# Mixture-of-experts blocks of 256, 192, 128 or 64 tokens, in nested branches, with two groups of TensorE's columns for the parts of 64

## The chip, the cores and the metric

The kernel runs on one core of one Trainium2 chip. The core has five instruction streams that run beside each other and meet through semaphores: TensorE (PE in the profile; its weight loads are listed as PEld), VectorE (DVE), ScalarE (ACT), GpSimd (POOL) and SyncE (SP). SyncE issues plain DMA transfers, GpSimd the indirect ones, which gather or scatter rows by a list of row numbers. The metric is the device time of one execution in microseconds (us). Before the change it was 790.62 us, the median of three runs (790.05 to 791.95).

## The reference

One block of a transformer with adaptive layer norm, all in float32, on 4 sequences of 1024 tokens of width D = 256 (T = 4096 tokens in all). The first half is a gated linear recurrence in place of attention, the second a mixture of E = 8 experts of hidden width F = 1024, of which each token uses its best two:

```python
def ffn(x, Wg, bg, W1, b1, W2, b2):
    gate_scores = softmax(x @ Wg + bg)
    topk_scores, topk_idx = top_k(gate_scores, 2)
    topk_scores = topk_scores / (sum(topk_scores) + 1e-08)
    combine_w = ...            # (tokens, E): the two scores at their experts, else 0
    for e in range(8):
        h = gelu(x @ W1[e] + b1[e])
        output += (h @ W2[e] + b2[e]) * combine_w[..., e:e+1]

h = layernorm(x) * (1 + ca) + sa
x = x + ga * recurrence(h)             # projections, associative scan, projection back
h = layernorm(x) * (1 + cb) + sb
x = x + gb * ffn(h)
```

The modulation rows sa, ca, ga, sb, cb, gb come from a small product of the condition c. Which tokens go to which expert is known only on the chip, after the gate.

## The kernel before

**First part, to about 301 us.** The sequences are worked through in eight chunks of 512 tokens (lines 1020 to 1116): norm, four projections (L417), scan, output projection (L454), the second norm and the gate (`f_gate`, L564, a product whose four groups of 32 tokens go to four groups of 32 columns of TensorE). The normalized rows and the gate rows `gb` are stored in a table `hx` in memory, the sum so far in the output. After each sequence the routing functions (`r_*`) find the two experts of each token and its rank within each expert. GpSimd scatters pairs (token, weight) into `lists` in memory, one region of T entries per expert, a few at a time (`drain`, L586).

**Blocks.** Each expert's list is cut into blocks of TK = 256 tokens; a block is two halves of 128 (HK = 2). There are up to NJ = 39 blocks. Which expert and which place of its list a block has stands in small tables that VectorE computes: `full_table` for blocks 0 to 7 and 8 to 15, which are certain to be whole, and `late_table` (L765) for the other 23. The late table has two segments of eight columns: first the whole blocks of each expert (a remainder of over 128 makes one more whole block), then a half block for each remainder of 1 to 128. `table` finds block i's segment by comparing its number with the running sum over all columns (operations on 23 x 16 elements). The two ends, the number of whole blocks and of all blocks, are loaded into registers of every engine as `n_whole` and `n_blocks`.

**Work of block j.** SyncE loads the entries of block j+3 (`fetch_entries`), GpSimd gathers the rows of block j+2 (`fetch_rows`, L830, three buffers `hb`), SyncE loads the expert's weights for block j+2 (`fetch_weights`: w1 and w2 of 1 MB each, two biases; three buffers, one of them in space freed by the first part, named proj and wo_sb in the profile). `b_up` (L917) makes h = gelu(w1 x + b1): 16 products on TensorE (L928; float32, each shows as two records in the profile), the gelu on ScalarE (L937). `b_turn` (L898) turns the next block's rows with 16 transposes on VectorE (L915), so that its up can start at once. `b_down` (L952) makes, for each half, 8 products with the hidden values as weights and w2 as the moving side (L958, 16 records); VectorE adds the bias (L972) and multiplies by the token's weight and gate row (L973), and GpSimd adds the rows to the output by a scatter (L945).

**Order.** The engines' order is the order of the code (the kernel is under a manual schedule, all engines). Blocks 0 to 27 (`sure_whole` = 28) are whole in any case and have no branch. From block 28 on, `work_either` (L1152) puts the whole form and the half form of a block into the two sides of an If on `n_whole` (compare-and-branch at L1153), and every engine has both sides in its program, one after the other. `sure` = 32 blocks exist in any case; beyond, `rest` (L1202) nests one If per block on `n_blocks` (L1203). `fetch_used` (L875) asks the same for block j+2's rows and weights. From block 31 on, a block's last part is kept back: its rows stay in `last_y` and their places in `last_at` (copied at L968), and the scatter is issued inside the next `rest`, or at the end. So this copy waits until the scatter of the block before has landed.

Of the kernel before, what the change touches and what calls it, by code (L numbers as in the profile page):

```python
# [9 lines left out]
F32 = mybir.dt.float32  # L10
# [9 lines left out]
def tile_adaln_block(  # L20
# [688 lines left out]
    def table(counts, starts, segments, n, what):  # L709
# [6 lines left out]
        past = small.tile([P, n, sg], F32, tag="past", name=f"past{what}", bufs=1)  # L716
# [18 lines left out]
        if sg > E:  # L735
            nc.vector.tensor_scalar(at, who, float(E), float(-E), ALU.is_ge, ALU.mult)
            nc.vector.tensor_add(who, who, at)
# [4 lines left out]
    counts2 = const.tile([P, 2, E], F32, tag="counts2", name="counts2")  # L742
    starts = const.tile([P, 2 * E + 1], F32, tag="starts", name="starts")
# [5 lines left out]
    nc.gpsimd.memset(starts[:, 2 * E :], float(E * BPE))  # L749
# [15 lines left out]
    def late_table():  # L765

        whole = blocks_of(float(P - 1), "lw")
        some = blocks_of(float(TK - 1), "ls")
        nc.vector.tensor_sub(counts2[:, 0, :], whole, done)
        nc.vector.tensor_sub(counts2[:, 1, :], some, whole)  # L770
        nc.vector.tensor_add(starts[:, E : 2 * E], starts[:, :E], counts2[:, 0, :])
        tab, cum = table(
            counts2.rearrange("p s e -> p (s e)"), starts, 2 * E, NJ - NM, "l"
        )
        ends_at = small.tile([P, 2], I32, tag="ends_at", name="ends_at", bufs=1)
        nc.vector.tensor_scalar_add(ends_at[:, 0:1], cum[:, E - 1 : E], float(NM))
        nc.vector.tensor_scalar_add(ends_at[:, 1:2], cum[:, 2 * E - 1 :], float(NM))
        return tab, ends_at
# [22 lines left out]
    def seen(j: int):  # L801

        return next((batches * S for n, batches, _ in TIERS if j < n), T)
# [71 lines left out]
    def fetch_used(j: int, half: bool):  # L875

        if j + 3 < NJ:
            fetch_entries(j + 3)

        def rest():  # L880
            fetch_rows(j + 2, half)
            fetch_weights(j + 2)

        if j + 2 < sure:
            rest()
        elif j + 2 < NJ:
            with tc.If(n_blocks > j + 2):
                rest()
# [28 lines left out]
    def b_up(j: int, half: bool = False):  # L917
        w1, bb, xT = (BK[j][n] for n in ("w1", "bb", "xT"))
        g = xpool.tile([P, FC, TK], F32, tag="g", name=f"g_{j}_{half}", bufs=1)
        BK[j]["g"] = g  # L920
        n = P if half else TK
        at_once = TB // n
        for f2 in range(FC // at_once):
            ph = ps_mm.tile([P, at_once, n], F32, tag="mm", name=f"ph_{j}_{f2}_{half}")
# [16 lines left out]
    last_y = xpool.tile([P, D], F32, tag="last_y", name="last_y", bufs=1)  # L941
    last_at = const.tile([P, 1], I32, tag="last_at", name="last_at")
# [9 lines left out]
    def b_down(j: int, half: bool = False, mid=None, keep: bool = False):  # L952

        g, w2, b2b, ent, hb = (BK[j][n] for n in ("g", "w2", "b2b", "ent", "hb"))
        for t in range(1 if half else HK):
            py = ps_y.tile([P, D], F32, tag="y", name=f"pye_{j}_{t}_{half}")
            for fc in range(FC):
                nc.tensor.matmul(  # L958
                    py,
                    lhsT=g[:, fc, ts(t, P)],  # L960
                    rhs=w2[:, fc, :],
                    start=(fc == 0),
                    stop=(fc == FC - 1),
                )
            kept_back = keep and t == (0 if half else HK - 1)
            if kept_back:
                yb, at = last_y, last_at
                nc.vector.tensor_copy(last_at, ent[:, t, 0:1])  # L968
            else:
                yb = xpool.tile([P, D], F32, tag="yb", name=f"yb_{j}_{t}_{half}", bufs=3)  # L970
                at = ent[:, t, 0:1]
            nc.vector.tensor_add(yb, py, b2b)  # L972
            nc.vector.scalar_tensor_tensor(  # L973
                yb, yb, ent[:, t, 1:2].bitcast(F32), hb[:, t, D:], ALU.mult, ALU.mult
# [5 lines left out]
            ins = add_rows(yb, at, seen(j))  # L980
# [162 lines left out]
    def work(j: int, half: bool = False, keep: bool = False):  # L1143
        if j >= sure_whole:
            fetch_used(j, half)
        b_up(j, half)
        if j + 1 < NJ:

            b_turn(j + 1, half)
        b_down(j, half, keep=keep)  # L1150

    def work_either(j: int, keep: bool = False):  # L1152
        with tc.If(n_whole > j) as whole:  # L1153
            work(j, False, keep)
        with whole.Else():
            work(j, True, keep)


    sure_whole = (2 * T - E * P) // TK
    sure = 2 * T // TK  # L1160
    for j in range(2, sure_whole):
# [31 lines left out]
    n_whole = nc.values_load(  # L1193
        ends_at[0:1, 0:1], min_val=sure_whole, max_val=NJ, skip_runtime_bounds_check_because=why
    )
    n_blocks = nc.values_load(
        ends_at[0:1, 1:2], min_val=sure, max_val=NJ, skip_runtime_bounds_check_because=why
    )
    for j in range(sure_whole, sure):
        work_either(j, j == sure - 1)  # L1200

    def rest(j: int):  # L1202
        with tc.If(n_blocks > j):  # L1203
            add_rows(last_y, last_at, T)
            work_either(j, True)
            if j + 1 < NJ:
                rest(j + 1)


    rest(sure)  # L1210
# [34 lines left out]
```

## Time and profile before

| | |
|---|---|
| time, median of three runs | 790.62 us (790.05 to 791.95) |
| the profiled execution's own time | 789.1 us |
| its span, first to last instruction | 787.4 us |
| TensorE busy | 772.8 us, 98% of the span |
| mean granted clock of TensorE | 0.997 of full speed |
| VectorE, ScalarE, GpSimd busy | 504.3, 241.7, 290.3 us |
| TensorE, last whole block (30) | 728.26 to 742.07 us |
| TensorE, five half blocks (31 to 35) | 742.07 to 777.6 us |
| last scatter, issued and landed | 778.93 and 782.65 us |

The profile is that of one execution. Its lines give the engine, the line of the kernel, the operation, what it writes and reads, the shape (partitions x elements) and the number of instructions or records. Names such as `ph_True` carry the flag `half`: True for a half block. The letter q behind an engine (PEldq, SPq) marks instructions of its sequencer: branches, semaphores, issues of DMAs. Queue q8 carries the instructions of TensorE, in packets of 16 KB, q14 those of other engines.

### The profile page before, as it was taken

How to read it: one execution, taken by the hardware profiler on the slowest of the kernel's cores; microseconds unless marked ns; L12 is line 12 of the kernel's file. 1: busy time of each engine (PE TensorE's matmuls, PEld its weight loads, DVE VectorE, ACT ScalarE, POOL GpSimd, SP SyncE). 2: the span in 40 equal slices, each digit the busy share in tenths (PEclk: the TensorE clock that was granted, in tenths of full speed). 3: DMA queues.
4: the chain of work that ended last, by engine and by line, in shares of the span. 5: the costliest groups of instructions: out<-in, count | busy, mean ns of one | idle time of the engine just before them, and what ended most of it. 6: DMA issues, size and time to landing. Idle time of an engine off the chain costs nothing.

```text
span 787.4 us, 10804 instructions
## 1 busy us (share of the span) xinstructions
PE 772.8 (98%) x3279; PEld 577.1 (73%) x3279; DVE 504.3 (64%) x1391; ACT 241.7 (31%) x560; POOL 290.3 (37%) x370
## 2 busy tenths in 40 slices
PE   8999999999999999999999999999999999999995
PEld 5455545454546557888888888888888888888994
DVE  5787877898789869767547453544536354453563
ACT  4434243534433343223222122221312222131231
POOL 2102010106142712456564564634434243343431
PEclk9999999999999999999999999999999999999998
DMA  8321334042313265799469898898878687885781
GB/s 296 95 70 47 116 102 142 23 127 86 100 55 113 55 185 183 241 328 258 73 161 206 249 247 253 245 294 223 235 211 230 186 235 217 218 232 167 221 264 25
DMA packets 116040, 138.13 MB, mean 175 GB/s; under 512 B 25782, under 2 KB 100090, under 8 KB 115968
## 3 DMA queue, kind: packets, MB, share of 16 engines
q1 hardware_dynamic: 97184, 111.46, 45.0%
q0 software_dynamic: 17216, 25.25, 15.9%
q10 hardware_dynamic: 1568, 0.57, 0.3%
q8 instruction: 32, 0.52, 0.3%
q14 instruction: 40, 0.33, 0.1%
HBM read 113.52 MB, written 25.42 MB: 176 GB/s over the span
## 4 chain that ended last, share of the span: by engine, by line
PE 83%; DMA 8%; DVE 4%; issue 2%; POOL 1%; ACT 1%; POOLq 0%; DVEq 0%
PE ph_False L928 25%; PE pye_False L958 23%; PE pya L454 7%; PE pk L417 6%; PE pgi L417 6%; PE pu L417 6%; PE pgo L417 6%; DMA hb<-hx,ent 5%; DMA out_dram<-yb_False,ent 2%; PE idle L263 1%; DMA proj<-in_L_ffn_W_dram 1%; PE pm L290 1%; PE pta L399 1%; PE pl L564 1%; DVE s L443 0%
## 5 line engine op out<-in xcount | busy, mean ns | idle before, releaser
L937 ACT ACTIVATE g_False<-ph_False,bb 128x256 f32<-128x256 f32 x248 | 103.8, 470 | 303.0 <-issue 188.2
L915 DVE STREAM_TRANSPOSE xT<-hb 32x128 f32<-32x128 f32 (+1 forms) x576 | 168.8, 293 | 12.7 <-DMA hb<-hx,ent 3.6
L958 PE MATMUL pye_False<-w,g_False 128*128 128x256 f32 x672 | 148.7, 379 | 0.0
L928 PE MATMUL ph_False<-xT,w 128*128 128x256 f32 x672 | 148.6, 379 | 0.0
L928 PEld LDWEIGHTS ph_False<-xT,w 128*128 128x128 f32 x672 | 127.4, 190 | 17.9 <-issue 0.7
L958 PEld LDWEIGHTS pye_False<-w,g_False 128*128 128x128 f32 x672 | 127.5, 190 | 17.6 <-issue 0.2
L945 POOL DMA_INDIRECT out_dram<-yb_False,ent x46 | 73.4, 1595 | 139.9 <-DVE yb_False L973 138.4
L972 DVE TENSOR_TENSOR yb_False<-pye_False,b2b 128x256 f32<-128x256 f32 x42 | 17.8, 424 | 126.3 <-PE pye_False L958 123.8
L586 POOL DMA_INDIRECT lists<-pay,placei x64 | 66.4, 1037 | 38.5 <-DMA ent<-lists 27.4
L928 PE MATMUL ph_False<-xT,proj 128*128 128x256 f32 x320 | 70.8, 379 | 0.7 <-DMA proj<-in_L_ffn_W_dram 0.7
L958 PE MATMUL pye_False<-proj,g_False 128*128 128x256 f32 x320 | 70.7, 379 | 0.0
L928 PEld LDWEIGHTS ph_False<-xT,proj 128*128 128x128 f32 x320 | 60.7, 190 | 9.3 <-DVE yb_False L972 1.0
L958 PEld LDWEIGHTS pye_False<-proj,g_False 128*128 128x128 f32 x320 | 60.8, 190 | 8.3
L830 POOL DMA_INDIRECT hb<-hx,ent x53 | 55.6, 1048 | 22.4 <-issue 15.6
L417 PE MATMUL pk<-hT,proj 128*128 128x512 f32 x128 | 61.0, 599 | 0.7 <-ACT hT L1015 0.7
L223 POOL TENSOR_TENSOR rstd_f<-rstd_f,expo 128x4 f32<-128x4 f32 x8 | 8.2, 1022 | 142.4 <-DVE rstd_f L222 98.8
L417 PE MATMUL pu<-hT,proj 128*128 128x512 f32 x128 | 60.2, 592 | 0.0
L417 PE MATMUL pgo<-hT,proj 128*128 128x512 f32 x128 | 60.2, 592 | 0.0
L417 PE MATMUL pgi<-hT,proj 128*128 128x512 f32 x128 | 60.2, 592 | 0.0
L454 PE MATMUL pya<-wo,z 128*128 128x256 f32 x256 | 56.8, 380 | 0.0
L454 PEld LDWEIGHTS pya<-wo,z 128*128 128x128 f32 x256 | 48.4, 190 | 8.6 <-issue 2.4
L972 DVE TENSOR_TENSOR yb_False<-pye_False,wo_sb 128x256 f32<-128x256 f32 x20 | 8.5, 424 | 60.4 <-PE pye_False L958 60.3
(234 smaller groups left out, 811.1 us busy)
## 6 DMA issues: line engine op xcount, KB each, us to landing
w<-in_L_ffn_W_dram SPq DMA_DIRECT2D x48, 1024.0 KB
proj<-in_L_ffn_W_dram SPq DMA_DIRECT2D x24, 1024.0 KB
hx<-gb SPq DMA_DIRECT2D x4, 1024.0 KB
out_dram<-x SPq DMA_DIRECT2D x8, 512.0 KB
hx<-h SPq DMA_DIRECT2D x8, 512.0 KB
x<-in_L_attn_x_dram SPq DMA_DIRECT2D x7, 512.0 KB
swapped<-u SPq DMA_DIRECT2D x7, 512.0 KB
hT<-swapped SPq DMA_DIRECT2D x28, 128.0 KB
```

The source lines that it names most:

```text
L223: nc.gpsimd.tensor_tensor(rstd, rstd, expo[:, 0, :], ALU.pow)
L263: nc.tensor.transpose(idle[:, :P], ident, ident)
L417: nc.tensor.matmul(ps, lhsT=w[:, k, col : col + P], rhs=hT[:, k, :], start=(k == 0), stop=(k == KC - 1),)
L454: nc.tensor.matmul(py[:, t, :], lhsT=z[hc][:, ts(2 * q + t, P)], rhs=wo[:, hc, :], start=(hc == 0), stop=(hc == HC - 1),)
L586: ins = nc.gpsimd.indirect_dma_start(out=lists[:, :], out_offset=IndirectOffsetOnAxis(ap=place, axis=0), in_=what, in_offset=None, bounds_ ...
L830: nc.gpsimd.indirect_dma_start(out=hb[:, t, :], out_offset=None, in_=hx[: seen(j), :], in_offset=IndirectOffsetOnAxis(ap=BK[j]["ent"][:, t ...
L915: nc.vector.transpose(to[ts(q, SQ), :, :, ts(i, SQ)], hb[ts(i, SQ), :, :, ts(q, SQ)])
L928: nc.tensor.matmul(ph[:, u, :], lhsT=w1[:, k, ts(fc, P)], rhs=xT[:, k, :n], start=(k == 0), stop=(k == KC - 1),)
L937: nc.scalar.activation(g[:, fc, :n], ph[:, u, :], AF.Gelu_apprx_tanh, bias=bb[:, fc : fc + 1])
L945: return nc.gpsimd.indirect_dma_start(out=out_rows[:n], out_offset=IndirectOffsetOnAxis(ap=at, axis=0), in_=yb, in_offset=None, bounds_che ...
L958: nc.tensor.matmul(py, lhsT=g[:, fc, ts(t, P)], rhs=w2[:, fc, :], start=(fc == 0), stop=(fc == FC - 1),)
L972: nc.vector.tensor_add(yb, py, b2b)
```

## The change

The blocks of the late table get four sizes, 256, 192, 128 and 64 tokens, instead of two. An expert's remainder takes the smallest size that holds it. The table has four segments of eight columns (its scratch space moves into spare columns of wo_sb), and four limits `n_upto` are loaded instead of two. `sure(k)` gives for each size the smallest and the largest value of its limit, (26, 33), (28, 35), (30, 37), (32, 39); branches start at block 26 instead of 28, and `work_any` nests one If for each further size that a block number may have: two sizes at 26 and 27, three at 28 and 29, four at 30 to 32, and fewer beyond. All sizes that are possible for a block stand in every engine's program one after the other, smaller ones behind larger ones; TensorE's program grows from 541 to 616 KB.

A block of 192 is a part of 128 and one of 64. For a part of 64 tokens the products of `b_down` alternate between PSUM's partitions 0 to 63 and 64 to 127, each by its own group of 64 columns of TensorE (`beside` = 2); a second addition on VectorE joins the two sums. Operations behind it work on 64 partitions. `last_y` is cleared once, early, since a part of 64 fills only half of it; in the scatter that is kept back the other rows go where `last_at` says.

```diff
         tab = small.tile([P, 2, n], I32, tag=f"tab{what}", name=f"tab{what}", bufs=1)
-        past = small.tile([P, n, sg], F32, tag="past", name=f"past{what}", bufs=1)
+        if what == "l":
+            past = wo_sb.rearrange("p c d -> p (c d)")[:, D : D + n * sg]
+            past = past.rearrange("p (n s) -> p n s", s=sg)
+        else:
+            past = small.tile([P, n, sg], F32, tag="past", name=f"past{what}", bufs=1)
         who = small.tile([P, n], F32, tag="who", name=f"who{what}", bufs=1)
...
         nc.vector.tensor_scalar_min(tab[:, 1, :], at, float(E * BPE))
-        if sg > E:
+        for _ in range(sg // E - 1):
             nc.vector.tensor_scalar(at, who, float(E), float(-E), ALU.is_ge, ALU.mult)
...
-    counts2 = const.tile([P, 2, E], F32, tag="counts2", name="counts2")
-    starts = const.tile([P, 2 * E + 1], F32, tag="starts", name="starts")
+    QT = P // 2
+    sizes = [TK, TK - QT, P, QT]
+    NS = len(sizes)
...
+    counts4 = const.tile([P, NS, E], F32, tag="counts4", name="counts4")
+    starts = const.tile([P, NS * E + 1], F32, tag="starts", name="starts")
     done = const.tile([P, E], F32, tag="done", name="done")
...
     nc.gpsimd.memset(starts[:, E : E + 1], float(E * BPE))
-    nc.gpsimd.memset(starts[:, 2 * E :], float(E * BPE))
+    nc.gpsimd.memset(starts[:, NS * E :], float(E * BPE))
...
-        whole = blocks_of(float(P - 1), "lw")
-        some = blocks_of(float(TK - 1), "ls")
-        nc.vector.tensor_sub(counts2[:, 0, :], whole, done)
-        nc.vector.tensor_sub(counts2[:, 1, :], some, whole)
-        nc.vector.tensor_add(starts[:, E : 2 * E], starts[:, :E], counts2[:, 0, :])
+        upto = [
+            blocks_of(float(TK - 1 - (sizes[k + 1] if k + 1 < NS else 0)), f"l{k}")
+            for k in range(NS)
+        ]
+        for k in range(NS):
+            nc.vector.tensor_sub(counts4[:, k, :], upto[k], upto[k - 1] if k else done)
+        for k in range(1, NS):
+            nc.vector.tensor_add(
+                starts[:, k * E : (k + 1) * E], starts[:, (k - 1) * E : k * E],
+                counts4[:, k - 1, :],
+            )
         tab, cum = table(
-            counts2.rearrange("p s e -> p (s e)"), starts, 2 * E, NJ - NM, "l"
-        )
-        ends_at = small.tile([P, 2], I32, tag="ends_at", name="ends_at", bufs=1)
-        nc.vector.tensor_scalar_add(ends_at[:, 0:1], cum[:, E - 1 : E], float(NM))
-        nc.vector.tensor_scalar_add(ends_at[:, 1:2], cum[:, 2 * E - 1 :], float(NM))
+            counts4.rearrange("p s e -> p (s e)"), starts, NS * E, NJ - NM, "l"
+        )
+        ends_at = small.tile([P, NS], I32, tag="ends_at", name="ends_at", bufs=1)
+        nc.vector.tensor_scalar_add(
+            ends_at, cum.rearrange("p (s e) -> p s e", e=E)[:, :, E - 1], float(NM)
+        )
         return tab, ends_at
...
-        if j + 2 < sure:
+        if j + 2 < sure_any:
             rest()
         elif j + 2 < NJ:
-            with tc.If(n_blocks > j + 2):
+            with tc.If(n_upto[-1] > j + 2):
                 rest()
...
-    def b_up(j: int, half: bool = False):
+    def b_up(j: int, n: int = TK):
         w1, bb, xT = (BK[j][n] for n in ("w1", "bb", "xT"))
-        g = xpool.tile([P, FC, TK], F32, tag="g", name=f"g_{j}_{half}", bufs=1)
+        g = xpool.tile([P, FC, TK], F32, tag="g", name=f"g_{j}_{n}", bufs=1)
         BK[j]["g"] = g
-        n = P if half else TK
-        at_once = TB // n
+        at_once = min(TB // n, FC // 2)
         for f2 in range(FC // at_once):
-            ph = ps_mm.tile([P, at_once, n], F32, tag="mm", name=f"ph_{j}_{f2}_{half}")
+            ph = ps_mm.tile([P, at_once, n], F32, tag="mm", name=f"ph_{j}_{f2}_{n}")
             for u in range(at_once):
...
     last_y = xpool.tile([P, D], F32, tag="last_y", name="last_y", bufs=1)
+    nc.gpsimd.memset(last_y, 0.0)
     last_at = const.tile([P, 1], I32, tag="last_at", name="last_at")
...
-    def b_down(j: int, half: bool = False, mid=None, keep: bool = False):
+    def b_down(j: int, size: int = TK, mid=None, keep: bool = False):
         g, w2, b2b, ent, hb = (BK[j][n] for n in ("g", "w2", "b2b", "ent", "hb"))
-        for t in range(1 if half else HK):
-            py = ps_y.tile([P, D], F32, tag="y", name=f"pye_{j}_{t}_{half}")
+        parts = [(0, min(size, P))] + ([(1, size - P)] if size > P else [])
+        for t, n in parts:
+            py = ps_y.tile([P, D], F32, tag="y", name=f"pye_{j}_{t}_{size}")
...
+            beside = P // n
             for fc in range(FC):
                 nc.tensor.matmul(
-                    py,
-                    lhsT=g[:, fc, ts(t, P)],
+                    py[ts(fc % beside, n), :],
+                    lhsT=g[:, fc, ds(t * P, n)],
                     rhs=w2[:, fc, :],
-                    start=(fc == 0),
-                    stop=(fc == FC - 1),
+                    start=(fc < beside),
+                    stop=(fc >= FC - beside),
                 )
-            kept_back = keep and t == (0 if half else HK - 1)
+            kept_back = keep and (t, n) == parts[-1]
             if kept_back:
...
             else:
-                yb = xpool.tile([P, D], F32, tag="yb", name=f"yb_{j}_{t}_{half}", bufs=3)
+                yb = xpool.tile([P, D], F32, tag="yb", name=f"yb_{j}_{t}_{size}", bufs=3)
                 at = ent[:, t, 0:1]
-            nc.vector.tensor_add(yb, py, b2b)
+            nc.vector.tensor_add(yb[:n], py[:n], b2b[:n])
+            if beside > 1:
+                nc.vector.tensor_add(yb[:n], yb[:n], py[n:])
             nc.vector.scalar_tensor_tensor(
-                yb, yb, ent[:, t, 1:2].bitcast(F32), hb[:, t, D:], ALU.mult, ALU.mult
+                yb[:n], yb[:n], ent[:n, t, 1:2].bitcast(F32), hb[:n, t, D:], ALU.mult, ALU.mult
             )
...
                 nc.gpsimd.memset(between, 0.0)
-            ins = add_rows(yb, at, seen(j))
+            ins = add_rows(yb[:n], at[:n], seen(j))
             for other in BK[j]["acc"]:
...
-    def work(j: int, half: bool = False, keep: bool = False):
-        if j >= sure_whole:
-            fetch_used(j, half)
-        b_up(j, half)
+    def sure(k: int):
...
+        less = sizes[k + 1] if k + 1 < NS else 0
+        return (
+            (2 * T - E * less) // TK,
+            max((2 * T - p * (less + 1)) // TK + p for p in range(E + 1)),
+        )
...
+    def work(j: int, size: int, keep: bool):
+        fetch_used(j, size <= P)
+        b_up(j, size)
         if j + 1 < NJ:
-            b_turn(j + 1, half)
-        b_down(j, half, keep=keep)
...
-    def work_either(j: int, keep: bool = False):
-        with tc.If(n_whole > j) as whole:
-            work(j, False, keep)
-        with whole.Else():
-            work(j, True, keep)
...
-    sure_whole = (2 * T - E * P) // TK
-    sure = 2 * T // TK
+            b_turn(j + 1, size <= P)
+        b_down(j, size, keep=keep)
...
+    def work_any(j: int, keep: bool):
...
+        able = [
+            k for k in range(NS) if j < sure(k)[1] and (k == 0 or j >= sure(k - 1)[0])
+        ]
...
+        def choose(i: int):
+            k = able[i]
+            if i == len(able) - 1:
+                work(j, sizes[k], keep)
+                return
+            with tc.If(n_upto[k] > j) as first:
+                work(j, sizes[k], keep)
+            with first.Else():
+                choose(i + 1)
...
+        choose(0)
...
+    sure_whole, sure_any = sure(0)[0], sure(NS - 1)[0]
+    assert sure(NS - 1)[1] == NJ
     for j in range(2, sure_whole):
...
-    n_whole = nc.values_load(
-        ends_at[0:1, 0:1], min_val=sure_whole, max_val=NJ, skip_runtime_bounds_check_because=why
-    )
-    n_blocks = nc.values_load(
-        ends_at[0:1, 1:2], min_val=sure, max_val=NJ, skip_runtime_bounds_check_because=why
-    )
-    for j in range(sure_whole, sure):
-        work_either(j, j == sure - 1)
+    n_upto = [
+        nc.values_load(
+            ends_at[0:1, k : k + 1], min_val=sure(k)[0], max_val=NJ,
+            skip_runtime_bounds_check_because=why,
+        )
+        for k in range(NS)
+    ]
+    n_blocks = n_upto[-1]
+    for j in range(sure_whole, sure_any):
+        work_any(j, j == sure_any - 1)
...
             add_rows(last_y, last_at, T)
-            work_either(j, True)
+            work_any(j, True)
             if j + 1 < NJ:
...
-    rest(sure)
+    rest(sure_any)
     add_rows(last_y, last_at, T)
```

## The prediction

> **What bounds the kernel now.** I read the page's busy shares first, then its chain, then the timeline of the last blocks, since the change acts only there.
>
> ```profile
> span 787.4 us, 10804 instructions
> PE 772.8 (98%) x3279; PEld 577.1 (73%) x3279; DVE 504.3 (64%) x1391; ACT 241.7 (31%) x560; POOL 290.3 (37%) x370
> q8 instruction: 32, 0.52, 0.3%
> PE 83%; DMA 8%; DVE 4%; issue 2%; POOL 1%; ACT 1%; POOLq 0%; DVEq 0%
> ```
>
> TensorE is busy for 98% of the span, and 83% of the chain runs through it: work taken from TensorE shortens the run, as long as nothing else gets late. The third line is TensorE's own program: 32 packets of 16 KB, read from memory while it runs. It returns below.
>
> The timeline of TensorE:
>
> ```profile
> 728.26 7.07 PE L928 MATMUL ph_False<-xT,w 128*128 128x256 f32 x32
> 735.16 7.07 PE L958 MATMUL pye_False<-w,g_False 128*128 128x256 f32 x32
> 742.07 3.73 PE L928 MATMUL ph_True<-xT,w 128*128 128x128 f32 x32
> 745.64 3.62 PE L958 MATMUL pye_True<-w,g_True 128*128 128x256 f32 x16
> ...
> 763.30 3.81 PE L928 MATMUL ph_True<-xT,w 128*128 128x128 f32 x32
> 766.95 3.62 PE L958 MATMUL pye_True<-w,g_True 128*128 128x256 f32 x16
> 770.41 3.73 PE L928 MATMUL ph_True<-xT,proj 128*128 128x128 f32 x32
> 773.98 3.62 PE L958 MATMUL pye_True<-proj,g_True 128*128 128x256 f32 x16
> ```
>
> Columns: start, length, group. From start to start a whole block takes 742.07 − 728.26 = 13.81 us (6.91 up, 6.90 down), a half block 7.0 (3.57 up, 3.5 down), with no gap between. The page has 672 + 320 = 992 up records of 256 columns, so 992/32 = 31 whole blocks (0 to 30), and five halves (31 to 35) follow; TensorE ends at 777.6. The span ends with two operations on VectorE (to 778.6), the last scatter (issued 778.93, landed 782.65) and 4.7 us of closing. The run took 789.1 us, 1.7 around the span; the median shown is 790.62, so 1.5 is added at the end.
>
> **Which blocks the inputs make.** The reference's routing with its own inputs gives the eight experts 1849, 1836, 484, 383, 1127, 837, 1258 and 418 entries; over multiples of 256 these leave 57, 44, 228, 127, 103, 69, 234 and 162. By the old rule 162, 228 and 234 make whole blocks and five remainders halves: 31 + 5, as the trace has it. By the new rule 162 makes one block of 192, the remainders 127, 103 and 69 make 128, and 57 and 44 make 64: 30 whole, 192 as block 30, 128 as 31 to 33, 64 as 34 and 35. Still 36 blocks, with the same weights to load.
>
> **Saved on TensorE.**
> Block 30, up: 32 records of 192 columns. One of 256 takes 216 ns from start to start, one of 128 takes 112; on the line between, 164 would give 5.2 us, so 1.7 is saved. Down, first part: unchanged, 3.45. Down, last 64 tokens: 16 records in two groups of columns. The nearest row is the gate's product, four groups of 32:
>
> ```profile
> 308.45 0.33 PE L673 MATMUL pr<-chose,before 128*128 128x64 f32 x2
> 308.62 0.39 PE L676 MATMUL pr<-earlier,ones 128*128 128x64 f32 x2
> 308.84 0.34 PE L680 MATMUL pr<-ended,ones 128*128 128x8 f32 x2
> 309.04 7.15 PE L454 MATMUL pya<-wo,z 128*128 128x256 f32 x32
> 316.12 0.64 PE L564 MATMUL pl<-hT,wg_sb 128*32 128x128 f32 x16
> 316.69 7.17 PE L958 MATMUL pye_False<-w,g_False 128*128 128x256 f32 x32
> ```
>
> Its 16 records take 0.64 us where one after another they would take 16 × 0.112 = 1.8: the groups do run together. Entering costs 316.12 − 315.81 (the last record's start) − 0.216 = 0.09, leaving 0.1. So the part takes 16 × 0.216 / 2 + 0.19 = 1.92 us instead of 3.45. Block 30 falls from 13.81 to 10.57: **3.24**. Bounds: 1.5 if the groups don't overlap, 3.4 if entering and leaving are free.
>
> Blocks 34 and 35, up with 64 columns: the rows above with 64 and with 8 columns both pass at 0.09 to 0.11 us a record (308.45, 308.62, 308.84, 309.04, two each), as 128 columns do: the weights' load sets it. So up saves nothing (bounds 0 and 1.7, if only columns counted). Down: 1.92 for 3.46. That is **1.54** each.
>
> [...]
>
> Sum on TensorE: 3.24 + 2 × 1.54 = **6.3 us**.
>
> **What does not shrink.** In blocks 34 and 35 VectorE is nearly as late as TensorE:
>
> ```profile
> 759.21 4.00 DVE L915 STREAM_TRANSPOSE xT<-hb 32x64 f32<-32x64 f32 x16 [1.00 <-DMA hb<-hx,ent]
> 764.55 0.15 DVE L968 COPY last_at<-ent 128x1 int32<-128x1 int32 x1 [1.35 <-DMA out_dram<-last_y,last_at]
> ```
>
> The turn of block 34 ends at 763.24 and its up starts at 763.30; the copy waits 1.35 for a scatter to land. A small block costs VectorE 4.0 (turn) + 0.15 + 0.42 + 0.48 = 5.05, plus 0.45 for the added second sum, or 5.5 with TensorE at 3.57 + 1.92 = 5.49. Block 35's result would come about 1.3 us, not 3.1, earlier than block 30's gain alone puts it: 3.24 + 1.3 ≈ **4.5 us**.
>
> Other edits. The bigger late table (L765; VectorE 429.6 to 435.05 now) gains about 3.8 us by its rows (two more counts at 0.49, sums at 0.2, four wide operations from 0.54 to 0.93): it ends near 439, while the buffer of sums that it holds up is next written at 445 and the turn of block 10 is due at 452; uncovered it would cost 3.8. Two more loads of limits (0.3 to 0.5 us each at 696.8) lie beside block 27's matmuls, and the added memset where POOL idles (8.9 to 13.6): nothing. Weights: the last w1 lands near 764, w2 by 769.2, wanted at 773.98 now and about 769.5 then: covered, but only just.
>
> **What is added: code to jump over.** A small block runs 6.3 KB of TensorE code. Now its untaken whole branch (8.4 KB) is jumped. Afterwards blocks 31 and 32 have the whole and the 192 body ahead (16.8 KB) and the 64 body behind (6.4): some 30 KB a block, 33 and 34 about 21, 35 about 13. In packets of 16 KB that is 1.85, 1.85, 1.35, 1.35, 0.8, sum 7.2, against about 5. The trace's records of the instruction queue show that a packet follows TensorE's entry into a new 16 KB, 1.0 to 1.9 us later when the queues are calm, 3.6 to 6.4 while weights flow (757 to 768). And what a jump costs:
>
> ```profile
> L1153 PEldq COMPARE_BRANCH  x11: 65/185/445, 697.8 to 768.5; - x11
> L1203 PEldq COMPARE_BRANCH  x6: 65/68/3697, 747.0 to 779.3; - x6
> ```
>
> (Shortest, middle, longest in ns.) Over 8.4 KB it costs 0.2 us; the one jump far ahead of what was read, 44 KB at the end, took **3.7 us**. TensorE's sequencer resumes when the last gelu has run, 2.1 us before TensorE runs out in a small block (3.9 in a whole one): this cover hides one calm packet, not two.
>
> My working, by packets: blocks 31 and 32 start with two packets, 2 × 1.45 − 2.1 = 0.8 each; block 33's comes behind the weights, 5.0 − 2.1 = 2.9; 34 and 35 start covered, but each crosses an edge while it runs with less than 1 us queued, 0.75 each. Sum 6.0. I add 0.45 for the second sum ahead of the last scatter and 0.5 for the same fetches of VectorE and SyncE (8 KB packets; bounds 0 and 1.5). Total −6.3 + 6.0 + 0.95 = **+0.65**: 789.75 in the profiled execution. The bounds of the fetch wait are 0, all hidden, and 15.4 (two packets at 3.7 for 31 and 32, 5.3 over the cover each, and three of 1.6).
>
> [...]
>
> **Rivals.**
> A (forecast): fetching eats what TensorE saves, 789.1 + 0.65. For it: 3.7 us where a jump left the read code; 30 KB a block. Against: the present jumps cost nothing visible. With the median's 1.5: **791.2**, own range 788 to 794.
> B: the fetches stay hidden under running matmuls, and 4.5 us are gained: 789.1 − 4.5 + 1.5 = **786.1**. For it: five small blocks now run without a gap, although each passes a new packet.
> C, slower: the reads at the starts of blocks 31 to 35 cost twice the above, 12 us, because the second can be asked for only after the first and both stand behind the weights: 789.1 − 6.3 + 12 + 0.95 + 1.5 = **797.3**. It decides from 8.7 us of waiting on, 6.3 and the 2.4 that 0.3% are. For it: 3.6 to 6.4 us per packet between 757 and 768; against: the weights for blocks 30 to 32 are in by then.
> D: the two groups don't overlap with 256 columns. Block 30 saves 1.5, 34 and 35 lose 0.2 each, less than 2.4 in all with hidden fetches: about **789.5**.
>
> **How the numbers follow.** A 0.55, B 0.20, C 0.20, D 0.05. 0.3% (2.4 us) is about what a measurement can tell from no change. A gives faster 0.05, same 0.33, slower 0.17; B faster 0.20; C slower 0.20; D same 0.05. So 0.25, 0.38 and 0.37. The range runs from just under B, 785.5, to about C, 797.0.
>
> **What would show it.** Saved work: block 30's first up matmul to block 31's at 10.6 us, up records of 192 columns at 162 to 165 ns, 16 half-width records in 1.9 us; up of 64 columns in 3.6. Fetching: gaps on TensorE ahead of blocks 31 to 33, ended by no DMA and no engine, with a compare-and-branch of TensorE of over 1 us, and about five more q8 packets. If those gaps are absent, A and C are wrong. If VectorE's turn or a scatter's landing ends the gaps instead, the tail that I credit with 4.5 us was mis-sized.

## The result, and the profile after

The changed kernel takes 801.87 us (median of four runs, 798.49 to 803.0) against 790.4, the median of four runs of the kernel before: a ratio of 1.0135, with a 95% interval of 1.0116 to 1.0154. It is 11.5 us slower where the forecast was 791.2 (0.65 us more), and lies above the range that was given (785.5 to 797.0). The profiled execution took 803.0 us.

The page of the changed kernel, the lines that answer to those of before:

```profile
span 801.2 us, 10898 instructions
PE 772.6 (96%) x3279; PEld 573.9 (72%) x3279; DVE 509.6 (64%) x1407; ACT 240.7 (30%) x560; POOL 290.6 (36%) x371
q8 instruction: 37, 0.61, 0.3%
PE 38%; DMA 26%; issue 17%; POOL 8%; DVE 7%; POOLq 1%; ACT 1%; SPq 0%; another core or an unknown queue 0%; DVEq 0%
```

TensorE's busy time is the same, 772.6 to 772.8: most of what its work lost in columns came back as slower work. The span is 13.8 us longer, so TensorE now idles. In the chain, "issue" (an engine that waits for nothing that the profile shows) went from 2% to 17%. TensorE read 37 packets of its program, not 32. The timeline of TensorE from block 30 on:

```profile
732.22 5.44 PE L943 MATMUL ph<-xT,w 128*128 128x192 f32 x32 [0.51 <-DVE yb L991]
737.50 5.49 PE L977 MATMUL pye<-w,g 128*128 128x256 f32 x32
745.51 3.81 PE L943 MATMUL ph<-xT,w 128*128 128x128 f32 x32 [2.52 <-issue]
...
755.05 3.81 PE L943 MATMUL ph<-xT,proj 128*128 128x128 f32 x32 [2.27 <-issue]
...
774.31 6.45 PE L943 MATMUL ph<-xT,w 128*128 128x64 f32 x32 [4.34 <-issue]
780.68 3.68 PE L977 MATMUL pye<-w,g 128*64 128x256 f32 x16
784.30 4.21 PE L943 MATMUL ph<-xT,proj 128*128 128x64 f32 x32
788.43 1.95 PE L977 MATMUL pye<-proj,g 128*64 128x256 f32 x16
```

The brackets hold the idle time before a group: 2.52 us ahead of block 31, 2.27 ahead of 32, 4.34 ahead of 34. Block 34 has the same work as block 35, yet its last product takes 3.68 us and block 35's 1.95. What holds TensorE is seen in the branches of `work_any` (L1191; shortest, middle, longest in ns). Why block 34 is slow is seen in the busy time of three stretches, in which the third number from the end is the granted clock of TensorE:

```profile
L1191 PEldq COMPARE_BRANCH  x25: 65/220/5362, 674.3 to 781.9; - x25
```

```profile
770.00:774.30 4.30, 0.00 (x0) 0.03 (x1) 2.90 (x11) 0.00 (x0) 1.58 (x1) 1.00 0.41 96
774.30:780.70 6.40, 6.39 (x34) 6.28 (x34) 2.05 (x10) 0.93 (x4) 0.00 (x0) 0.55 0.07 8
780.70:784.30 3.60, 3.60 (x18) 1.71 (x17) 0.00 (x0) 0.93 (x4) 0.00 (x0) 0.50 0.02 5
```

One branch takes 5.36 us; the trace's records have five over 0.5 us there, at 728.03 (3.52), 741.42 (3.14), 750.55 (0.64), 751.67 (2.73) and 768.23 (5.36). In each of the four long ones one packet of queue 8 is read (from 729.22, 742.11, 751.98 and 771.13, about 1 us each), and the branch ends 1.3 to 1.5 us after it. The first matmul follows 0.65 to 0.95 us later, ahead of block 30 too, where the bracket names an operation of VectorE: that branch ends at 731.55, the block starts at 732.22. From 774.97 the clock is granted at half for 10.24 us, through block 34 and into 35.

TensorE is behind before all that. It is level with the kernel before until block 9 and 3.2 us late at block 11:

```profile
453.49 7.14 PE L943 MATMUL ph<-xT,w 128*128 128x256 f32 x32 [1.17 <-DMA w<-in_L_ffn_W_dram]
...
469.02 6.28 PE L943 MATMUL ph<-xT,proj 128*128 128x256 f32 x28 [1.48 <-DMA proj<-in_L_ffn_W_dram]
```

These two waits for weights come just behind the longer late table on VectorE. So there are three suspects: reads of the program at jumps (theory F, with the half clock as a consequence), the late table (theory T), and the small parts themselves (rival W); for T the rival is chance (N), for F that a test costs by itself (G).

### The profile page after: what moved, and what is told of

It is laid out like the page before. It is cut to its first block, busy times and chain, and to the rows that moved or that the text cites. A ratio compares the mean times of both kernels' runs of the same rounds, so it can differ in the third digit from the quotient of the medians.

```text
span 801.2 us, 10898 instructions
## 1 busy us (share of the span) xinstructions
PE 772.6 (96%) x3279; PEld 573.9 (72%) x3279; DVE 509.6 (64%) x1407; ACT 240.7 (30%) x560; POOL 290.6 (36%) x371
## 4 chain that ended last, share of the span: by engine, by line
PE 38%; DMA 26%; issue 17%; POOL 8%; DVE 7%; POOLq 1%; ACT 1%; SPq 0%; another core or an unknown queue 0%; DVEq 0%
DMA out_dram<-yb,ent 15%; PE pk L417 5%; POOL out_dram L961 5%; PE pya L454 5%; PE ph L943 5%; PE pgi L417 5%; PE pu L417 5%; PE pgo L417 5%; DMA lists<-pay,placei 5%; PE pye L977 4%; DMA ent<-lists 3%; DMA out_dram<-last_y,last_at 2%; POOL lists L586 1%; DVE s L443 1%; PE idle L263 1%
## 5 line engine op out<-in xcount | busy, mean ns | idle before, releaser
L952 ACT ACTIVATE g<-ph,bb 128x256 f32<-128x256 f32 (+3 forms) x288 | 114.2, 452 | 345.9 <-issue 183.8
L943 PE MATMUL ph<-xT,w 128*128 128x256 f32 (+3 forms) x768 | 161.3, 369 | 8.9 <-issue 7.2
L943 PEld LDWEIGHTS ph<-xT,w 128*128 128x128 f32 x768 | 140.2, 195 | 27.7 <-issue 8.9
L977 PE MATMUL pye<-w,g 128*128 128x256 f32 (+1 forms) x720 | 158.0, 385 | 0.0
L977 PEld LDWEIGHTS pye<-w,g 128*128 128x128 f32 (+1 forms) x720 | 133.1, 190 | 19.9 <-issue 1.5
L961 POOL DMA_INDIRECT out_dram<-yb,ent x46 | 73.3, 1593 | 136.5 <-DVE yb L994 133.8
L943 PE MATMUL ph<-xT,proj 128*128 128x256 f32 (+2 forms) x384 | 78.9, 364 | 4.5 <-issue 2.3
L586 POOL DMA_INDIRECT lists<-pay,placei x64 | 67.0, 1047 | 40.3 <-DMA ent<-lists 28.7
L943 PEld LDWEIGHTS ph<-xT,proj 128*128 128x128 f32 x384 | 68.4, 192 | 14.6 <-issue 3.4
L977 PE MATMUL pye<-proj,g 128*128 128x256 f32 (+1 forms) x352 | 76.3, 379 | 0.0
L977 PEld LDWEIGHTS pye<-proj,g 128*128 128x128 f32 (+1 forms) x352 | 64.8, 188 | 9.1
```

Of the source, the lines that this page charges most:

```text
L586: ins = nc.gpsimd.indirect_dma_start(out=lists[:, :], out_offset=IndirectOffsetOnAxis(ap=place, axis=0), in_=what, in_offset=None, bounds_ ...
L943: nc.tensor.matmul(ph[:, u, :], lhsT=w1[:, k, ts(fc, P)], rhs=xT[:, k, :n], start=(k == 0), stop=(k == KC - 1),)
L952: nc.scalar.activation(g[:, fc, :n], ph[:, u, :], AF.Gelu_apprx_tanh, bias=bb[:, fc : fc + 1])
L961: return nc.gpsimd.indirect_dma_start(out=out_rows[:n], out_offset=IndirectOffsetOnAxis(ap=at, axis=0), in_=yb, in_offset=None, bounds_che ...
L977: nc.tensor.matmul(py[ts(fc % beside, n), :], lhsT=g[:, fc, ds(t * P, n)], rhs=w2[:, fc, :], start=(fc < beside), stop=(fc >= FC - beside),)
```

## The experiments

Ratios are to the kernel before on the same chip, with their 95% intervals.

### First: table, branches and work taken apart

**table_only**: the kernel before with `table` and `late_table` of the changed one, whose limits leave the segments of 192 and 64 empty.

```diff
-        whole = blocks_of(float(P - 1), "lw")
-        some = blocks_of(float(TK - 1), "ls")
...
+        upto = [
+            blocks_of(float(P - 1 if k < 2 else TK - 1), f"l{k}")
+            for k in range(NS)
+        ]
...
```

> The kernel before, with the late table of four segments (the segments of 192 and 64 get no block), and nothing else of the change. In the changed kernel TensorE is level with the old one until block 9 (0.17 us behind) and 3.2 us behind at block 11, after two waits for weights, right behind the longer table. Theory T: the table does this, since VectorE reaches block 8's first sum 4.5 us later, and GpSimd's scatter, gathers and all transfers move behind it. It expects about 3 us more than before, 793.5, with waits of TensorE ahead of blocks 10 and 11. Rival N: the waits for weights are chance of the transfers. It expects at most 0.5 us, 790.9.

Measured: 1.0023 (1.0005 to 1.0042), some 1.8 us. A wait of 2.06 us for weights stands ahead of block 10, none ahead of block 11. The interval, 0.4 to 3.3 us, leaves T's 3 us possible and nearly reaches N's 0.5; the wait speaks for T.

**split**: the changed kernel, the table in three steps (`late_table` hands back control after each third).

```diff
-        elif j == NE:
-            tab["l"], ends_at = late_table()
+        elif j == NE:
+            late = late_table()
+            next(late)
+        elif j == NE + 1:
+            next(late)
...
```

> The changed kernel, with the late table made in three steps on VectorE, behind the turns of blocks 9, 10 and 11, each short enough for the 4.4 us that VectorE idles there. Theory T expects 3 us less than the changed kernel, about 798.8, and no wait ahead of blocks 10 and 11. Rival N expects no difference, about 801.9.

Measured: 1.0073 (1.0050 to 1.0096), and no wait ahead of blocks 10 and 11. Both kernels were run again side by side, since the first two ratios were not taken together:

**after_again** (no edit) and **split_again** (the same edit):

> The changed kernel, once more, beside the same with its late table in steps, on one chip and against the same runs of before. Its first ratio was 1.0135, with waits for weights of 1.2 and 1.5 us ahead of blocks 10 and 11 and half clock in blocks 34 and 35. Theories T (table) and F both expect 1.011 to 1.015 and the wait ahead of block 10 again.

> The changed kernel with the late table in three steps, once more (1.0073 before, from another chip's call). Theory T expects 0.003 to 0.005 less than the changed kernel of this call, and no wait ahead of block 10. Rival N expects no difference within the intervals.

Measured: 1.0130 (1.0113 to 1.0148) and 1.0071 (1.0049 to 1.0093). The split is worth 0.006, 4.7 us, more than T expected. Over all runs, the five profiles with the long table in one piece (the changed kernel twice, table_only, no_if, same_work) have a wait of 1.2 to 2.6 us for weights ahead of block 10, and none of the others has. T holds; its size was 1.8 us in one pair of kernels and 4.7 in the other, and stays open.

**no_if**: the changed kernel with the inputs' sizes in the program. It leaves out the choice at run time.

```diff
+    LAST = 36
...
-    n_upto = [
...
-    for j in range(sure_whole, sure_any):
-        work_any(j, j == sure_any - 1)
...
+    SIZE = {30: 192, 31: 128, 32: 128, 33: 128, 34: 64, 35: 64}
+    for j in range(sure_whole, LAST):
+        if j >= sure_any:
             add_rows(last_y, last_at, T)
...
+        work(j, SIZE.get(j, TK), j >= sure_any - 1)
```

> The changed kernel, with the sizes of these inputs' blocks written into the program (192 for block 30, 128 for 31 to 33, 64 for 34 and 35, 36 blocks): no branch, no jump and no loads of limits; the choice at run time is left out, the work on the data is the same. Theory F: the gaps of 2 to 4 us ahead of blocks 31, 32 and 34 are TensorE's program being read after a jump, and the half clock of blocks 34 and 35 follows from the longest gap. It expects no such gap, full clock, block 34 at 5.5 us from start to start, and a time of 790.4 - 4.5 + 3 (late table) = 789, within 1.5. Rival W: the small parts are slow by themselves (64 columns, two groups, the second sum). It expects block 34 near 10 us again, and at least 794.

Measured: 0.9967 (0.9955 to 0.9980), which is 787.8 against the 790.4 of the result: inside F's 789 ± 1.5, far from W's 794. Its timeline of TensorE:

```profile
731.36 5.36 PE L943 MATMUL ph<-xT,w 128*128 128x192 f32 x32
736.56 5.49 PE L977 MATMUL pye<-w,g 128*128 128x256 f32 x32
741.98 3.84 PE L943 MATMUL ph<-xT,w 128*128 128x128 f32 x32
...
763.17 3.68 PE L943 MATMUL ph<-xT,w 128*128 128x64 f32 x32
766.78 1.95 PE L977 MATMUL pye<-w,g 128*64 128x256 f32 x16
768.65 3.79 PE L943 MATMUL ph<-xT,proj 128*128 128x64 f32 x32
772.37 1.95 PE L977 MATMUL pye<-proj,g 128*64 128x256 f32 x16
```

No bracket: no gap. Block 30 takes 741.98 − 731.36 = 10.62 us, block 34 takes 5.48: the sizes do what they should, and rival W falls.

**same_work**: the changed kernel, with the limits of table_only. All bodies and tests are there, none of 192 or 64 is ever taken.

> The changed kernel with all its branches and bodies, but with limits that give the old blocks (31 whole, five of 128, none of 192 or 64): the work is that of the kernel before. Theory F: only the code that is jumped over counts, so the gaps stay, 2 to 5 us ahead of two to four of the blocks 31 to 35 and perhaps the half clock: 790.4 + 3 (late table) + 8 to 14, that is 801 to 807. Rival W: without small parts there are no gaps: 793.5.

Measured: 1.0084 (1.0065 to 1.0102), 796.88. The work of the kernel before, and three branches of 3.0 to 3.6 us:

```profile
744.20 3.81 PE L943 MATMUL ph<-xT,w 128*128 128x128 f32 x32 [0.63 <-DVE yb L991]
...
753.75 5.44 PE L943 MATMUL ph<-xT,proj 128*128 128x128 f32 x32 [2.28 <-issue]
...
772.07 5.44 PE L943 MATMUL ph<-xT,w 128*128 128x128 f32 x32 [2.40 <-issue]
```

Up of 128 takes 5.3 us after the last two in place of 3.6: half clock for 3.4 us. W, which had no gaps here, is refuted again. F is right in kind; its 8 to 14 us were too many, since 0.0084 less the table's 0.0023 leaves 4.8.

### Second: what the work is worth without branches

**no_if_split** and **no_if_two**: no_if with the table in steps; then with two buffers for the rows and places kept back.

```diff
-                yb, at = last_y, last_at
+                yb, at = lasts[j % 2]
```

> The kernel with the sizes written into the program and no branch (ratio 0.9967 to before), with the late table in three steps on VectorE besides. Its own trace still had a wait of 2.6 us for weights ahead of block 10, and 3.4 us of half clock behind it (block 10's up took 8.7 us in place of 6.9). Theory T (the longer table delays the transfers): both go, 4 us less, a ratio near 0.992. Rival N (chance of the transfers): the wait stays, 0.9967.

> No branches, late table in three steps, and two buffers for the kept-back rows and their places in turn. Without the second buffer (ratio 0.9959) TensorE was early by 4 us at block 30, and then block 35 waited 2.8 us and ran at half clock: the copy of the places on VectorE waited 3.6 us for the landing of the scatter before, and block 35's turn stood behind it. Theory B (the one buffer does it): the copy waits no more, block 35 starts without a gap and at full clock, 4 us less: 0.991. Rival D (the transfers themselves are late, at 100% of their engines from 752 to 764): the turn waits for gathered rows instead, within 1 us of the kernel without the buffer, 0.995 to 0.997.

Measured: 0.9959 (0.9941 to 0.9978) and 0.9923 (0.9906 to 0.9940). The first is near N's figure, yet not for N's reason: its wait at block 10 is gone, as T has it, and a new one came ahead of block 35, where VectorE's turn stood behind the copy of `last_at`:

```profile
764.21 0.15 DVE L997 COPY last_at<-ent 128x1 int32<-128x1 int32 x1 [3.56 <-DMA out_dram<-last_y,last_at]
```

```profile
767.21 6.72 PE L953 MATMUL ph<-xT,proj 128*128 128x64 f32 x32 [2.82 <-DVE xT L941]
773.86 3.68 PE L987 MATMUL pye<-proj,g 128*64 128x256 f32 x16
```

A scatter issued at 757.02 had landed 7.2 us later, with the transfers at 98 to 100% of their engines. After the wait of 2.8 us block 35 ran at half clock (0.50 granted from 768 to 776 us). With the second buffer both are gone (theory B). 0.0077 of 790, **6.1 us, is what the smaller sizes are worth** without branches, with the second buffer and the table in steps.

### Third: what the branches' cost goes by

**split_192**, **split_64**, **split_shared**: the changed kernel with the table in steps, and fewer bytes of code: without 64, without 192 (`sizes = [TK, P, QT]`), or with one body up to the hidden values for 128 and 64 and a test behind it. The edit of split_192:

```diff
-    sizes = [TK, TK - QT, P, QT]
+    sizes = [TK, TK - QT, P]
```

> The changed kernel with the late table in three steps, and without the size of 64: 256, 192 and 128, block 30 of 192, 31 to 35 of 128. Theory F (reads of the program at jumps): a block of 128 now has 16.8 KB to jump and 6.3 to run, 23 KB in place of 30, so that a jump mostly ends in the 16 KB after the present ones; gaps of 2 to 3 us at one block or none instead of three. Saved 3.2 at block 30, so 0.996 without a gap, 0.999 with one. Rival G (any third body costs as much as a fourth, the gap coming with each nested test): three gaps as in the changed kernel, 2.5 us each, ratio 1.006.

> The same without the size of 192: 256, 128 and 64, blocks 0 to 30 whole, 31 to 33 of 128, 34 and 35 of 64. Per block of 128: 14.7 KB to jump and 6.3 to run, 21 KB. Theory F: gaps at one block or none; saved 1.5 + 1.3, so 0.9965 without a gap and 0.9995 with one. Rival G: three gaps, 1.006.

> All four sizes with the late table in three steps, but blocks of 128 and of 64 share one body up to the hidden values (64 columns cost TensorE as much as 128 there), and a test behind it chooses the last product alone. A block passes 25 KB of TensorE code in place of 30. Theory F: between the three sizes and the four, one or two gaps, ratio 0.995 to 1.002. Rival G: one more test per block, three gaps or more, 1.006 or above.

Measured: 1.0013 (0.9993 to 1.0033), 1.0023 (1.0004 to 1.0043), 1.0000 (0.9980 to 1.0020). The first two lie between F's figure for one gap (0.999, 0.9995) and G's 1.006, the third in F's range. The traces decide between them: branches of over 1 us on TensorE ahead of blocks are two, one and two, in place of the four of the changed kernel, and gaps ahead of blocks 31 to 35 with such a branch are one in each, where G had three. In split_64 the branch takes 5.83 us (a gap of 4.75), with the DMA engines busy at 96% and more until its packet came, and half clock follows for 6.8 us.

**three_order**, **three_order_two**, **four_order_two**: the body of 192 moved behind the others, so that a block of 128 after it has little to jump; the last two with the second buffer.

```diff
+            if sizes[k] == TK - QT:
+                with tc.If(n_upto[k] <= j) as less:
+                    choose(i + 1)
+                with less.Else():
+                    work(j, sizes[k], keep)
+                return
```

> Three sizes (256, 192, 128) and the late table in steps as before (ratio 1.0013), but the body of 192 stands behind that of 128, so that after block 30 (192) only the whole body of block 31 is jumped (8.4 KB) and not 6.3 + 16.8. Theory F expects the gap of 2.3 us ahead of block 31 to go, and none elsewhere over 1 us: 0.998. Rival G (each nested test costs, wherever its body stands): 1.0013 as before.

> The same with the two buffers of the kernel without branches. Theories F and B: both gaps go, 3.2 us saved at block 30 stay: 0.996. Rivals G and D: 1.000 or above.

> All four sizes in the order 256, 128, 64, 192, table in steps, two buffers. Theory F: no gap ahead of block 31 (8.4 KB to jump), but 23 KB between blocks of 128 and 30 KB ahead of block 34, so one or two gaps of 2 to 4 us: 0.998 to 1.003. Rival G: the three gaps of the changed kernel, 1.005 or above.

Measured: 0.9999 (0.9983 to 1.0015), 1.0005 (0.9991 to 1.0018), 1.0122 (1.0103 to 1.0141). F expected 0.998, 0.996 and at most 1.003: it missed all three, and the figures are G's. The traces say more. In three_order the gap ahead of block 31 went from 2.28 to 0.56, as F has it, but a new one of 3.0 us came ahead of block 32, where 16.8 KB are jumped: the mechanism held, F's count of where reads fall did not. four_order_two has three gaps over 2 us, as G had it: 4.56 ahead of block 30, 2.03 ahead of block 33 and 2.52 inside block 34. A packet of TensorE's program is read in each of them or just before it, and half clock follows twice for 6.8 us. The order moves a read, it doesn't remove it. The second buffer gained nothing here.

**down_only**, **down_192**, **down_64**: hidden values for 256 or 128 only; a test behind them chooses a last part of 128 or of 64. Table in steps, two buffers.

```diff
+        def either(n: int, t: int):
+            full, less = t * P + P in able, t * P + QT in able
+            if full and less:
+                with tc.If(n_upto[sizes.index(t * P + P)] > j) as more:
+                    b_part(j, t, P, keep)
+                with more.Else():
+                    b_part(j, t, QT, keep)
...
```

> All four sizes, but the hidden values are made for 256 or for 128 tokens only, and a second test behind them chooses between a last part of 128 and one of 64 (two groups of columns); table in steps, two buffers. As many tests per block as in the changed kernel, but only about 12.6 KB of TensorE code to jump between blocks of 128 in place of 23. Saved on TensorE: 1.54 at each of blocks 30, 34 and 35, 4.6 in all, less 0.45 for the second sum at the end. Theory F (bytes jumped): no gap over 1 us, ratio 0.995 to 0.997. Rival G (number of tests): gaps as in the changed kernel, 1.003 or above.

> The same without the size of 64: saved 1.54 at block 30 alone, 10.5 KB of code to jump per block of 128. Theory F: no gap, 0.998. Rival G: gaps at the tests, 1.002 or above.

> The same without the size of 192: saved 1.54 at blocks 34 and 35, less 0.45. Theory F: no gap, 0.997. Rival G: 1.002 or above.

Measured: 1.0028 (1.0002 to 1.0054), 0.9997 (0.9985 to 1.0009), **0.9967 (0.9954 to 0.9981)**. The branches, from the profile and the trace:

| kernel | TensorE's branches from 690 us on | over 1 us, ahead of a block | packets of its program |
|---|---|---|---|
| before | 27 | none | 32 |
| changed | 38 | 3.52, 3.14, 2.73, 5.36 | 37 |
| same_work | 39 | 3.19, 3.04, 3.64 | 37 |
| split_192 | 30 | 2.96, 3.03 | 34 |
| down_192 | 31 | none | 31 |
| split_64 | 34 | 5.83 | 33 |
| down_64 | 34 | none | 31 |
| down_only | 39 | 2.98 | 32 |
| no_if | 0 | none | 26 |

About equal numbers of branches (30 and 31, 34 and 34, 38 and 39) go with very different waits: rival G falls. That the long ones wait for code is in the records: the profiles of all runs have 43 branches of over 1 us on TensorE, in 42 exactly one packet of its program is read, and the branch ends 1.2 to 1.5 us behind that packet (the last one starts 0.3 us behind a packet). F's mechanism stands; its count of bytes was a rough measure only. In down_64 TensorE's branches take 0.45 us at most, and the one gap, 0.60 us, is a wait of its sequencer for VectorE's turn:

```profile
L1224 PEldq COMPARE_BRANCH  x10: 65/186/447, 697.7 to 761.0; - x10
```

```profile
763.44 3.81 PE L953 MATMUL ph<-xT,w 128*128 128x128 f32 x32 [0.60 <-issue]
767.18 1.95 PE L995 MATMUL pye<-w,g 128*64 128x256 f32 x16
769.05 3.84 PE L953 MATMUL ph<-xT,proj 128*128 128x128 f32 x32
772.82 1.95 PE L995 MATMUL pye<-proj,g 128*64 128x256 f32 x16
```

down_only misses F's figure (0.995 to 0.997). It still has one long branch, and in its profile block 35 waited 4.07 us for gathered rows that took 8 us to land, and ran at half clock (0.64 granted from 776 to 784 us). That profile is of one of its four slower runs (795.4 to 798.0); the other eight lie from 788.7 to 790.2, level with the kernel before and not under it.

**old_two_b**: the kernel before with the second buffer alone. Its first form, old_two, gave no time: the second buffer left 33.88 KB per partition for the weights, which need 34.09. So in old_two_b the late table's scratch space is moved as in the changed kernel.

> The kernel before with two buffers for the kept-back rows and their places (the scratch space of the late table moved as in the changed kernel, for room), nothing else of the change: what the second buffer is worth by itself. Only block 34 waited in the kernel before, 0.14 us, so both theories expect 0.999 to 1.001; a ratio near 0.997 would say that the gain of the variant with parts of 64 is the buffer's, and not the parts'.

Measured: 0.9995 (0.9987 to 1.0004). So the gain of down_64 is not the buffer's by itself. Its profile, the slowest of its twelve runs, has a gap of 2.29 us ahead of block 35, marked "issue", without a long branch: TensorE's sequencer waits 3.79 us there for VectorE's turn, which starts at 767.49, 8.3 us after the gather of its rows was issued. So "issue" alone does not prove a read of code; the branch and the packet do. The table in steps was not tried alone on the kernel before, but that one has no wait ahead of block 10 for it to take away. down_64 at 786.63 us beats the kernel before (789.39 beside it) and the changed one, with all choices made at run time.

## Why the prediction was wrong

**Saved work: right.** Block 30 took 10.77 us without the gap behind it, where 10.57 was worked out; records of 192 columns go at 165 ns (164 estimated); the part of 64 takes 1.95 (1.92), so the two groups do overlap and rival D falls; blocks 34 and 35 without stalls take 5.48 and 5.67 in no_if (5.49). no_if_two turns this into 6.1 us, near the 6.3 of the sum.

**Where the reads hurt: half right. Their price: wrong; this is the step that failed.** It was "by packets: blocks 31 and 32 start with two packets, 2 × 1.45 − 2.1 = 0.8 each". The 1.45 us was the delay from TensorE's entry into a block of code to the start of its packet. A jump that has to wait pays more: in the four long branches 0.3 to 2.9 us until the packet starts, 1 us for the packet, 1.3 to 1.5 from its end to the end of the branch, 2.7 to 5.4 in all, and 0.65 to 0.95 more to the first matmul. Against this stood a cover of 1.1 to 1.7 us at blocks 31, 32 and 34 (from the branch's start until TensorE ran out; for block 31, 1.57: 3.14 − 1.57 + 0.95 = 2.52). The row for this was in the page read: 3.70 us, shown and then used only for the upper bound. Ahead of blocks 30, 31, 32 and 34 and inside 33 TensorE lost 0.67 + 2.52 + 2.27 + 4.34 + 0.36 = 10.2 us in place of 6.0. The five more packets came as worked out, and blocks 31 and 32 were named rightly; the 2.9 us at block 33's start and the wait at 35 did not come, and 34 paid 4.34 in place of 0.75.

The 10.2 us are near rival C's price of 12, but C's reason is not what is seen: each long branch reads one packet, not two in turn. By itself the price would have given 789.1 − 6.3 + 10.2 + 0.95 + 1.5 = 795.5, inside the range. Not every jump waits: in the kernel before, those of 8.4 KB took 0.2 us, and none of its branches at L1153 over 0.45. Of the starts of blocks 31 to 35 three paid a wait of over 2 us, 2.52 + 2.27 + 4.34 = 9.1 us.

**Half clock: not thought of.** Blocks 34 and 35 took 9.99 and 6.08 us in place of 5.48 and 5.67, 4.9 us more, because the clock stood at half after the gap ahead of block 34 (0.50 granted from 774.97 to 785.21). The prediction counted a gap once.

**The late table: wrong.** The prediction had 3.8 us for the longer table and called them covered; "the buffer of sums that it holds up is next written at 445" looked at TensorE alone. VectorE's first sum of block 8 came 4.5 us later, at 439.54 in place of 435.05. GpSimd's scatter of these rows moved from 436.26 to 440.76, and the next pair of the lists (L586), queued behind it, from 438.17 to 442.66. SyncE's load of entries waits for that, in the kernel before (first line) as in the changed one; the waits of its queue from 436 to 452 us (total, times, longest):

```profile
SPq L822 <- DMA lists<-pay,placei: 8.5, 1, 8.5
SPq L838 <- DMA lists<-pay,placei: 19.8, 2, 10.3
```

The load was issued at 445.61 in place of 443.10, and block 10's weights, next in SyncE's queue, at 446.86 in place of 444.15. That is the wait of 1.17 us at 453.49; the table in steps takes it away. TensorE was 3.3 us late from block 11 on. The second wait, 1.48 us ahead of block 11, was there in one profile of the five; why is open.

The sum of the profiled execution: −6.2 (sizes) + 10.2 (reads) + 4.9 (clock) + 3.3 (table) = 12.2 of the 12.8 us by which TensorE ends later; 1.0 more lies behind it, half of it the second sum ahead of the last scatter. This execution was the slowest of its four; in after_again's, its fastest, the gaps ahead of and inside blocks 31 to 34 come to 7.2 us. The tail, 4.5 in place of 6.3, was right in kind: without a second buffer, no_if_split lost its gain at block 35. The reads of VectorE and SyncE (0.5) leave no sign in their branches: from 600 us on, none of another engine than TensorE takes over 0.07 us in the changed kernel.

## What to carry to other kernels

In these kernels a choice at run time cost by the code that TensorE had to jump over, and not by the test (split_192: 30 branches, two of them of 3.0 us ahead of blocks; down_192: 31, none): keep the alternatives small and put the test where only the differing part lies behind it. Where a read falls was not foretold well by counting bytes, so look for long branches with a packet in them. Price a stall of TensorE with what follows it, here often a stretch of 3.4 to 10.2 us at half clock. And before an operation is called covered, follow every engine that stands behind it, not only the bottleneck.

## What the runs showed of the hardware

TensorE's granted clock fell to 0.50 after many short gaps. The stretches at half clock, while blocks were still worked on, were 3.4, 6.8 or 10.2 us long in the profiles. In the blocks, of 21 gaps of 1.79 to 3.00 us ahead of a product with 128 or 256 columns, eleven were followed by 3.4 us at half clock (the shortest 1.89, split_again) and ten by none (the longest 3.00, three_order). After the four gaps over 4 us it was 6.8 or 10.2. Five gaps of 1.8 us (split) to 2.8 us (no_if_split) stood ahead of a product with 64 columns: four were followed by 6.8 us, the longest by 10.2; why the clock came back later there is open, since no run varied the columns alone. In the changed kernel it stayed at half for 10.24 us, though TensorE's records followed each other without a gap (6.39 us busy of 6.40 in the stretch shown above).

A jump that waited for a packet of TensorE's program took 2.6 to 5.8 us. The two longest, 5.36 and 5.83, waited for their packet while the DMA engines were busy at 96% and more. Two groups of 64 columns beside each other run in parallel with 256 columns moving: 16 records in 1.95 us, where the same number in whole columns takes 3.62.
